# Product keys in eight stages instead of five, with every engine's order written out

## The chip, the cores and the metric

The kernel runs on one core of a Trainium2 chip. The core has five engines that work side by side, each through its own list of instructions in order: PE (TensorE, matmuls and transposes), DVE (VectorE), ACT (ScalarE), POOL (GpSimd), and SP (SyncE), which here only issues transfers. Instructions on different engines wait for each other by semaphores. The metric is the device time of one execution in microseconds (us), lower is better. Matmuls write to a memory of their own, PSUM, of eight banks; all other tiles stand in SBUF.

## The reference

A model of four layers, each a gated cross attention and a gated feed-forward block, on 16 sequences of 128 tokens and width 256. All arithmetic is in float32. The change lies in the last block, a feed-forward layer of product keys:

```
q  = batch_norm(x @ Wq + bq)            # 8 heads x (2 halves of 32)
q0, q1 = l2norm(first half), l2norm(second half)
s0, s1 = q0 . k0, q1 . k1               # 32 scores each
ts0, ti0 = top_k(s0, 4);  ts1, ti1 = top_k(s1, 4)
w  = softmax over all 16 sums ts0[i] + ts1[j]
idx = ti0[i] * 32 + ti1[j]              # one of 256 experts
out = sum over heads and pairs of  up[idx] * w * gelu(down[idx] . x)
```

All 16 pairs are kept, so the softmax over the sums is the product of two softmaxes, one over the four best of each half. Indices that would reach past the 256 experts (first index 8 or more) use the last expert.

## The kernel before

The kernel works on 16 tiles of 128 tokens (one sequence each). The last block is `attention_ffn3` (L1178). It first computes all queries, their batch-norm statistics, and `eh`, the gelu of every expert's down product, for all tiles. That ends with `gain` and `shift` (L1277 to L1280). Then comes the part that is changed: a loop over the 16 tiles.

For one tile `b` it does the following. ACT makes the squares and the normalised queries of four blocks (L1293, L1294). PE sums the squares by head half (`pn`, L1297), DVE copies the 16 sums out of PSUM (`rn`, L1299), and POOL takes the root with a power instruction and keeps it from zero (L1300, L1301). PE multiplies the queries with the keys (`ps`, L1304), and ACT copies the 16 x 32 scores to one of three score tiles (L1306). DVE inverts the norms (L1313); ACT takes 16 exps, one for each head half, with the inverted norm as the scale (`wgt`, L1316).

The four best of 32 scores are found on DVE in two steps for each of the 16 head halves. The eight largest come from a maximum instruction (L1320). The places 4 to 7 are overwritten by one memset with a value that stands behind the scores (L1321). Then a match instruction (L1324) marks, in a copy `rep`, where the remaining values stand. A scalar_tensor_tensor (L1328) keeps the exps at the marked places and zeroes the others.

Then the weights: sums over each half (`tot`, L1330), their reciprocal (L1331), the product of both halves' reciprocals (`both`, L1335), the scaled first eight weights of the first half (`w0`, L1337; the profile calls it `w`), the sum of the other 24 (`far`, L1339), scaled (L1340), and summed over the heads (`rest`, L1342). POOL multiplies `w0` with the 32 weights of the second half, for 8 heads x 8 x 32 products (`pr`, L1344). PE adds the eight heads by multiplying with the identity (`we`, L1355, with `rest` put to the last expert, L1359). DVE multiplies with `eh` (`ew`, L1361). PE turns the result (L196), ACT copies it (`eT`, L197), PE applies the up weights (`po`, L1369), DVE adds it with the gate to the tile (L236), and SP writes the tile out (L1371).

The loop is written as five stages a tile apart: `score(t)`, `pick(t - 2)`, `mix(t - 3)`, `apply(t - 4)`. In this loop a planner orders the instructions of each engine by when it expects their inputs, so the order on the chip is not that of the source. Other loops of the kernel already stand in a block where each engine takes its instructions in the order of the source, for PE, ACT, DVE and POOL (L613).

Of the kernel before, what the change touches and what calls it, by code (L numbers as in the profile page):

```python
# [12 lines left out]
F32 = mybir.dt.float32  # L13
I32 = mybir.dt.int32
BF16 = mybir.dt.bfloat16
AF = mybir.ActivationFunctionType
# [3 lines left out]
P = 128  # L20
B, S, D = 16, 128, 256
NH = 16
NG, GT = 4, 512
ENGINES = {mybir.EngineType.PE, mybir.EngineType.Activation, mybir.EngineType.DVE, mybir.EngineType.Pool}
# [9 lines left out]
def flamingo_gated(ctx: ExitStack, tc: tile.TileContext, a, out):  # L34
    nc = tc.nc
# [9 lines left out]
    def bank(name):  # L45
        return psum.tile([P, 512], F32, tag="ps", name=name)
# [20 lines left out]
    def gate_f(layer):  # L67
        return gates[:, 4 + layer : 5 + layer]
# [123 lines left out]
    def transposed(src, dst):  # L192

        pt = bank("pt")
        for c in range(2):
            nc.tensor.transpose(pt[:, c * P : (c + 1) * P], src[:, c * P : (c + 1) * P], ident)  # L196
        nc.scalar.copy(dst, pt[:, 0:256].rearrange("p (c t) -> p c t", c=2))  # L197

    class Norm:
# [17 lines left out]
        def turn(self, b):  # L217
            transposed(self.rows.pop(b), self.into(b))
# [16 lines left out]
    def add_gated(b, ps, gate):  # L235
        nc.vector.scalar_tensor_tensor(xb[b], ps, gate, xb[b], ALU.mult, ALU.add)  # L236
# [941 lines left out]
    def attention_ffn3():  # L1178
        norm, xnT = norm_stage()
        attention3(after=[norm.whole])  # L1180
        with ExitStack() as es:
            kp = es.enter_context(tc.tile_pool(name="pk", bufs=1))
            pp = es.enter_context(tc.tile_pool(name="pw", bufs=2))
# [3 lines left out]
            wu = wt[:, 1536:2048].rearrange("p (c m) -> p c m", c=2)  # L1187
# [13 lines left out]
            blk = kp.tile([P, 4], F32, name="blk")  # L1201
# [30 lines left out]
            for g in range(NG):  # L1232
                q = kp.tile([P, 4, GT], F32, tag=f"q{g}", name=f"q{g}")
                for c in range(4):
                    pq = bank("pq")
                    for k in range(2):
                        nc.tensor.matmul(  # L1237
                            pq, lhsT=wq[:, k, c * P : (c + 1) * P], rhs=xnT[g][:, k, :], start=(k == 0), stop=(k == 1)
# [10 lines left out]
            for b in range(B):  # L1249
                pe = bank("pe")  # L1250
                for k in range(2):
                    nc.tensor.matmul(
                        pe[:, 0:D], lhsT=xnT[b // 4][:, k, b % 4 * S : (b % 4 + 1) * S], rhs=wd[:, k, :],
                        start=(k == 0), stop=(k == 1),
                    )
                t = kp.tile([P, D], F32, tag=f"eh{b}", name="eh")
# [18 lines left out]
            gain = kp.tile([P, 1], F32, name="gain")  # L1275
            rsqrt(gain, var, 1e-5)
            nc.vector.tensor_tensor(gain, gain, par[:, 4:5], ALU.mult)  # L1277
            shift = kp.tile([P, 1], F32, name="shift")
# [4 lines left out]
            scored = [kp.tile([P, 16, 36], F32, tag=f"sc{i}", name=f"sc{i}") for i in range(3)]  # L1283
            for t in scored:
                nc.gpsimd.memset(t[:, :, 32:36], SENT)
            raw, norms, picked, mixed = {}, {}, {}, {}

            def score(b):

                q = qT[b // 4][:, :, (b % 4) * S : (b % 4 + 1) * S]  # L1290
                both = ctxp.tile([P, 2, 4, S], F32, tag="ctxT", name="both")
                q2, qn = both[:, 0], both[:, 1]
                nc.scalar.activation(q2, q, AF.Square, bias=shift, scale=gain)  # L1293
                nc.scalar.activation(qn, q, AF.Identity, bias=shift, scale=gain)  # L1294
                pn = bank("pn")
                for c in range(4):
                    nc.tensor.matmul(pn[:, c * 4 : (c + 1) * 4], lhsT=q2[:, c, :], rhs=blk, start=True, stop=True)  # L1297
                rn = pp.tile([P, 16], F32, tag="rn", name="rn", bufs=3)
                nc.vector.tensor_copy(rn, pn[:, 0:16])  # L1299
                nc.gpsimd.tensor_tensor(rn, rn, half.to_broadcast([P, 16]), ALU.pow)  # L1300
                nc.gpsimd.tensor_scalar(rn, rn, 1e-12, 1.0, ALU.max, ALU.mult)  # L1301
                ps = bank("ps")
                for c in range(4):
                    nc.tensor.matmul(ps[:, c * P : (c + 1) * P], lhsT=qn[:, c, :], rhs=kdT, start=True, stop=True)  # L1304
                sc = scored[b % 3]
                nc.scalar.copy(sc[:, :, 0:32], ps.rearrange("p (g k) -> p g k", k=32))  # L1306
                raw[b], norms[b] = sc, rn

            def pick(b):


                rn, sc = norms.pop(b), raw.pop(b)
                nc.vector.reciprocal(rn, rn)  # L1313
                w = pp.tile([P, 16, 32], F32, tag="wgt", name="wgt", bufs=3)
                for h in range(16):
                    nc.scalar.activation(w[:, h, :], sc[:, h, 0:32], AF.Exp, scale=rn[:, h : h + 1])  # L1316

                best = pp.tile([P, 16, 8], F32, tag="best", name="best")
                for h in range(16):
                    nc.vector.max(out=best[:, h, :], in_=sc[:, h, :])  # L1320
                nc.vector.memset(best[:, :, 4:8], SENT)  # L1321
                rep = pp.tile([P, 16, 36], F32, tag="rep", name="rep", bufs=1)
                for h in range(16):
                    nc.vector.match_replace(  # L1324
                        out=rep[:, h, :], in_to_replace=best[:, h, :], in_values=sc[:, h, :], imm_value=FOUND
                    )

                nc.vector.scalar_tensor_tensor(w, rep[:, :, 0:32], FOUND, w, ALU.is_equal, ALU.mult)  # L1328
                tot = pp.tile([P, 16], F32, tag="tot", name="tot")
                nc.vector.tensor_reduce(tot, w, AX.X, ALU.add)  # L1330
                nc.vector.reciprocal(tot, tot)  # L1331
                wv = w.rearrange("p (h s) k -> p h s k", s=2)
                tv = tot.rearrange("p (h s) -> p h s", s=2)
                both = pp.tile([P, 8], F32, tag="both", name="both")
                nc.vector.tensor_tensor(both, tv[:, :, 0], tv[:, :, 1], ALU.mult)  # L1335
                w0 = pp.tile([P, 8, 8], F32, tag="w0", name="w0")
                nc.vector.tensor_tensor(w0, wv[:, :, 0, 0:8], both.unsqueeze(2).to_broadcast([P, 8, 8]), ALU.mult)  # L1337
                far = pp.tile([P, 8], F32, tag="far", name="far")
                nc.vector.tensor_reduce(far, wv[:, :, 0, 8:32], AX.X, ALU.add)  # L1339
                nc.vector.tensor_tensor(far, far, tv[:, :, 0], ALU.mult)  # L1340
                rest = pp.tile([P, 1], F32, tag="rest", name="rest", bufs=3)
                nc.vector.tensor_reduce(rest, far, AX.X, ALU.add)  # L1342
                pr = pp.tile([P, 8, 8, 32], F32, tag="pr", name="pr")
                nc.gpsimd.tensor_tensor(  # L1344
                    pr, w0.unsqueeze(3).to_broadcast([P, 8, 8, 32]),
                    wv[:, :, 1, :].unsqueeze(2).to_broadcast([P, 8, 8, 32]), ALU.mult,
                )
                picked[b] = pr, rest

            def mix(b):  # L1350

                pr, rest = picked.pop(b)
                we = bank("we")
                for h in range(8):
                    nc.tensor.matmul(  # L1355
                        we[:, 0:D], lhsT=ident, rhs=pr[:, h].rearrange("p i k -> p (i k)"), start=(h == 0), stop=(h == 7)
                    )
                    if h == 0:
                        nc.tensor.matmul(we[:, D - 1 : D], lhsT=ident, rhs=rest, start=False, stop=False)  # L1359
                ew = pp.tile([P, D], F32, tag="ew", name="ew")  # L1360
                nc.vector.tensor_tensor(ew, eh[b], we[:, 0:D], ALU.mult)  # L1361
                mixed[b] = ew

            def apply(b):
                eT = pp.tile([P, 2, P], F32, tag="eT", name="eT")
                transposed(mixed.pop(b), eT)
                po = bank("po")
                for k in range(2):
                    nc.tensor.matmul(po[:, 0:D], lhsT=eT[:, k, :], rhs=wu[:, k, :], start=(k == 0), stop=(k == 1))  # L1369
                add_gated(b, po[:, 0:D], gate_f(3))  # L1370
                nc.sync.dma_start(out=out[b], in_=xb[b])  # L1371

            for t in range(B + 4):
                if 2 <= t < B + 2:
                    pick(t - 2)
                if t < B:
                    score(t)
                if 3 <= t < B + 3:
                    mix(t - 3)
                if t >= 4:  # L1380
                    apply(t - 4)


    def attention1(after, joining):
# [43 lines left out]

    attention_ffn2(attention_ffn1(attention_ffn0()))
    attention_ffn3()  # L1430


# [94 lines left out]
```

## Time and profile before

| | |
|---|---|
| median of 3 runs | 2210.04 us (2206.56 to 2211.8) |
| the profiled execution | 2212.79 us |
| its span in the trace | 2211.1 us |
| first square of the changed loop (L1293) | 2034.53 us |
| mean TensorE clock over the span | 0.936 |
| busy over the span: PE, DVE, ACT, POOL | 1948.9, 1291.9, 957.7, 769.3 us |

The page shows the whole program, of which the changed loop is the last 176.6 us. The busy times of the page are therefore of little use here; the loop has to be read from a window over its own stretch. In lines of a group or of the timeline, `rn<-pn` means that tile `rn` is written and `pn` read; x16 is the number of instructions, and an arrow in brackets names what ended the engine's idle time before the instruction. Where a query gives three durations, they are the shortest, the median and the longest in ns.

### The profile page before, as it was taken

The page shows a single profiled execution, that of the slowest core. Times are in us where ns is not written, and L with a number is a line of the kernel's source. Part 1 is how long each engine was busy: PE and PEld are TensorE (multiplying, and loading weights), DVE is VectorE, ACT ScalarE, POOL GpSimd, SP SyncE. Part 2 cuts the span into 40 slices and gives each one's busy share as a digit, 9 for nine tenths or more (in the row PEclk, how much of TensorE's full clock was granted, in tenths as well). Part 3 has the DMA queues.
Part 4 walks back from the last instruction along what each step waited for, and adds up shares of the span by engine and source line. Part 5 has one row for each costly group of instructions (what it writes and reads, how often), then busy time and mean ns, then how long its engine had stood idle before and what let it go on. Part 6 is the DMA issues. An engine that isn't in the chain of part 4 may idle for free.

```text
span 2211.1 us, 31775 instructions
## 1 busy us (share of the span) xinstructions
PE 1948.9 (88%) x10603; PEld 1319.0 (60%) x10603; DVE 1291.9 (58%) x3965; ACT 957.7 (43%) x3103; POOL 769.3 (35%) x921
## 2 busy tenths in 40 slices
PE   5996999888859999978887998949899999988787
PEld 4774566566645666655664444438776777765676
DVE  3776122267773222227766999859926667652775
ACT  5884222288851122228872111134424344434662
POOL 3653333255430145535543222200011222221675
PEclk9998999989879999999998999979999999999788
DMA  2002777511012288873002113543210000000000
GB/s 91 33 23 80 301 293 294 179 37 34 26 30 88 98 311 320 314 261 122 25 18 108 67 76 143 189 168 114 77 39 1 11 11 1 20 2 0 8 13 20
DMA packets 56563, 223.48 MB, mean 101 GB/s; under 512 B 11984, under 2 KB 31952, under 8 KB 44240
## 3 DMA queue, kind: packets, MB, share of 16 engines
q0 software_dynamic: 15312, 134.10, 16.6%
q1 hardware_dynamic: 41088, 87.36, 11.4%
q8 instruction: 84, 1.38, 0.3%
q14 instruction: 79, 0.65, 0.1%
HBM read 190.24 MB, written 31.20 MB: 100 GB/s over the span
## 4 chain that ended last, share of the span: by engine, by line
PE 25%; DVE 19%; POOL 4%; issue 4%; ACT 3%; DMA 1%; POOLq 0%; ACTq 0%; SPq 0%; DVEq 0%
PE pk L266 3%; PE pq L278 2%; PE po L361 2%; PE pv L289 2%; DVE tot L1135 2%; POOL rn L1300 2%; PE po L1155 2%; DVE d L1082 1%; DVE red L1079 1%; DVE tot L1086 1%; PE av L351 1%; DVE cw L1129 1%; PE sc L308 1%; PE pq L1237 1%; DVE cw L1137 1%
## 5 line engine op out<-in xcount | busy, mean ns | idle before, releaser
L803 PE MATMUL pg<-we,xT 128*128 128x512 f32 (+1 forms) x588 | 268.2, 586 | 1.0 <-ACT xT L197 1.0
L538 POOL TENSOR_TENSOR e<-e,sums 128x512 f32<-128x512 f32 x192 | 194.1, 1043 | 144.4 <-DVE sums L533 106.9
L809 DVE TENSOR_TENSOR h<-sg,pg 128x256 f32<-128x256 f32 x147 | 60.3, 411 | 248.0 <-ACT sg L808 201.8
L808 ACT ACTIVATE sg<-pg 128x256 f32<-128x256 f32 x147 | 55.3, 376 | 303.0 <-PE pg L803 295.5
L525 ACT ACTIVATE e<-sc,mx 128x128 f32<-128x128 f32 x512 | 179.7, 413 | 0.0
L803 PEld LDWEIGHTS pg<-we,xT 128*128 128x128 f32 x588 | 106.2, 192 | 89.1 <-issue 79.1
L778 POOL DMA_INDIRECT we<-in_we,rows x62 | 60.0, 967 | 264.3 <-PE pd L834 172.7
L834 PE MATMUL pd<-we,hT 128*128 128x256 f32 (+1 forms) x588 | 141.7, 383 | 1.2 <-ACT hT L823 1.2
L329 POOL TENSOR_TENSOR e<-e,rec 128x512 f32<-128x512 f32 x64 | 65.3, 1041 | 216.7 <-DVE rec L328 140.3
L834 PEld LDWEIGHTS pd<-we,hT 128*128 128x128 f32 (+1 forms) x588 | 109.6, 190 | 44.1 <-issue 25.8
L1155 PE MATMUL po<-yt,cT 128*128 128x256 f32 x512 | 128.2, 396 | 8.5 <-ACT cT L1147 8.4
L1098 PE MATMUL acc<-d,k 128*128 128x512 f32 x256 | 122.4, 620 | 9.7 <-POOL d L1088 9.5
L525 ACT ACTIVATION_READ_ACCUMULATOR e<-sc,mx 128x1 f32 x512 | 129.4, 253 | 0.0
L1088 POOL TENSOR_TENSOR d<-d,tot 128x1024 f32<-128x1024 f32 x32 | 62.8, 1961 | 168.4 <-DVE tot L1087 168.4
L494 PE MATMUL sc<-kT,qT 32*128 32x256 f32 x768 | 98.3, 432 | 25.0 <-DVE v L438 14.0
L1083 ACT ACTIVATE d<-d 128x1024 f32<-128x1024 f32 x32 | 33.8, 1057 | 195.5 <-DVE d L1082 189.2
L1072 PE MATMUL pl<-phi,xnT 128*128 128x512 f32 x256 | 116.5, 599 | 0.0
L544 PE MATMUL pe<-ident,e 128*128 128x128 f32 x768 | 104.1, 289 | 10.4 <-POOL e L538 10.2
L1155 PEld LDWEIGHTS po<-yt,cT 128*128 128x128 f32 x512 | 97.4, 200 | 21.4 <-ACT cT L1147 9.7
L180 POOL TENSOR_SCALAR ve<-mv 128x1 f32<-128x1 f32 (+1 forms) x136 | 26.1, 192 | 234.2 <-DVE mv L187 183.4
L544 PEld LDWEIGHTS pe<-ident,e 128*128 128x128 f32 x768 | 92.0, 152 | 17.2 <-POOL e L538 15.5
L236 DVE SCALAR_TENSOR_TENSOR x<-po,gates,x 128x256 f32<-128x256 f32 x96 | 45.4, 473 | 91.5 <-PE po L361 53.2
(291 smaller groups left out, 4538.4 us busy)
## 6 DMA issues: line engine op xcount, KB each, us to landing
ew<-in_ew SPq DMA_DIRECT2D x8, 2048.0 KB
spill<-lg SPq DMA_DIRECT2D x32, 512.0 KB
cw<-spill SPq DMA_DIRECT2D x8, 2048.0 KB
ctxT<-in_ctxT SPq DMA_DIRECT2D x16, 512.0 KB
got<-results SPq DMA_DIRECT2D x48, 128.0 KB
normed<-xn SPq DMA_DIRECT2D x32, 128.0 KB
aw<-in_aw SPq DMA_DIRECT2D x3, 1280.0 KB
x<-in_x SPq DMA_DIRECT2D x16, 128.0 KB
```

What stands on the lines that cost most here:

```text
L266: nc.tensor.matmul(pk, lhsT=wk[:, k, c * P : (c + 1) * P], rhs=ctxT[g][:, k, :], start=(k == 0), stop=(k == 1))
L329: nc.gpsimd.tensor_tensor(e, e, rec.unsqueeze(2).to_broadcast([P, 4, S]), ALU.mult)
L494: nc.tensor.matmul(banks[j][:, c * 256 : (c + 1) * 256].rearrange("p (i k) -> p i k", i=2), lhsT=qT[r, c, tok], rhs=kT[r, c, :, tok], star ...
L525: nc.scalar.activation(e[:, c, :], sc[:, c, :], AF.Exp, bias=mx[:, h : h + 1], scale=sign, accum_out=sums[b][:, h : h + 1],)
L538: nc.gpsimd.tensor_tensor(e, e, r, ALU.mult)
L544: nc.tensor.transpose(pe[:, c * P : (c + 1) * P], e[:, c, :], ident)
L803: nc.tensor.matmul(pg[:, 0 : 2 * m].rearrange("p (g i) -> p g i", g=2), lhsT=tokens[j][:, k, :], rhs=wgu[:, k, :, i0 : i0 + m], start=(k = ...
L834: nc.tensor.matmul(pd[:, 0:D], lhsT=hT[0:m, ic, :], rhs=wd[0:m, ic, :], start=(ic == 0), stop=(ic == nic - 1))
L1072: nc.tensor.matmul(pl, lhsT=xnT[b // 4][:, k, tok], rhs=phi[:, k, n], start=(k == 0), stop=(k == 1))
L1088: nc.gpsimd.tensor_tensor(dv, dv, tot.unsqueeze(2).to_broadcast([P, 32, 32]), ALU.mult)
L1098: nc.tensor.matmul(acc[hf][k][q], lhsT=keep[b][:, k * P : (k + 1) * P], rhs=d[:, q * 512 : (q + 1) * 512], start=(b == 0), stop=(b == B - 1),)
L1155: nc.tensor.matmul(pos[b][:, 0:D], lhsT=cT[:, c, :], rhs=yt[2 * q + c // 2][:, c % 2, :], start=(q == 0 and c == 0), stop=(q == 3 and c == 3),
```

## The change

The loop's four functions become eleven, which run up to seven turns apart, and the loop is put in a block in which PE, ACT, DVE and POOL each take their instructions in the order of the source. In turn `t` a stage with lag `k` works on tile `t - k`. The order of the table is the order in the turn.

Nothing is computed differently. `score` is split into `square`, `norm_sums`, `root` and `products`; `pick` into `exps`, `best_four` and `weigh`; `apply` into `turn`, `project` and `leave`. `rep`, in which the four best are marked, gets two buffers in place of one, `best` one in place of two, and `wgt` two in place of three. In `weigh` the instructions from L1328 to the end of `pick` are kept in their order of the source.

```diff
-            def score(b):
+            def square(b):
...
+            def norm_sums(b):
...
                 nc.vector.tensor_copy(rn, pn[:, 0:16])
+                norms[b] = rn
+
+            def root(b):
+                rn = norms[b]
                 nc.gpsimd.tensor_tensor(rn, rn, half.to_broadcast([P, 16]), ALU.pow)
                 nc.gpsimd.tensor_scalar(rn, rn, 1e-12, 1.0, ALU.max, ALU.mult)
+
+            def products(b):
...
-            def pick(b):
-                rn, sc = norms.pop(b), raw.pop(b)
+            def exps(b):
+                rn = norms.pop(b)
                 nc.vector.reciprocal(rn, rn)
-                w = pp.tile([P, 16, 32], F32, tag="wgt", name="wgt", bufs=3)
+                w = pp.tile([P, 16, 32], F32, tag="wgt", name="wgt")
...
+            def best_four(b):
+                sc = raw.pop(b)
-                best = pp.tile([P, 16, 8], F32, tag="best", name="best")
+                best = pp.tile([P, 16, 8], F32, tag="best", name="best", bufs=1)
...
-                rep = pp.tile([P, 16, 36], F32, tag="rep", name="rep", bufs=1)
+                rep = pp.tile([P, 16, 36], F32, tag="rep", name="rep")
...
+            def weigh(b):
+                w, rep = found.pop(b)
                 nc.vector.scalar_tensor_tensor(w, rep[:, :, 0:32], FOUND, w, ALU.is_equal, ALU.mult)
...
-            for t in range(B + 4):
-                if 2 <= t < B + 2:
-                    pick(t - 2)
-                if t < B:
-                    score(t)
-                if 3 <= t < B + 3:
-                    mix(t - 3)
-                if t >= 4:
-                    apply(t - 4)
+            stages = (
+                (2, root), (6, turn), (3, exps), (7, leave), (4, weigh), (1, norm_sums), (1, products),
+                (3, best_four), (5, mix), (6, project), (0, square),
+            )
+            with tc.manual_schedule(engines=ENGINES):
+                for t in range(B + 7):
+                    for lag, stage in stages:
+                        if 0 <= t - lag < B:
+                            stage(t - lag)
```

More of the change, by code (lines that the diff above doesn't have):

```diff
@@ L1285, in attention_ffn3 @@
                 nc.gpsimd.memset(t[:, :, 32:36], SENT)
-            raw, norms, picked, mixed = {}, {}, {}, {}
-            def score(b):
+            squares, norms, raw, found, picked, mixed, turned, outs = {}, {}, {}, {}, {}, {}, {}, {}
+            def square(b):
                 q = qT[b // 4][:, :, (b % 4) * S : (b % 4 + 1) * S]
                 both = ctxp.tile([P, 2, 4, S], F32, tag="ctxT", name="both")
-                q2, qn = both[:, 0], both[:, 1]
-                nc.scalar.activation(q2, q, AF.Square, bias=shift, scale=gain)
-                nc.scalar.activation(qn, q, AF.Identity, bias=shift, scale=gain)
+                nc.scalar.activation(both[:, 0], q, AF.Square, bias=shift, scale=gain)
+                nc.scalar.activation(both[:, 1], q, AF.Identity, bias=shift, scale=gain)
+                squares[b] = both
+            def norm_sums(b):
                 pn = bank("pn")
                 for c in range(4):
-                    nc.tensor.matmul(pn[:, c * 4 : (c + 1) * 4], lhsT=q2[:, c, :], rhs=blk, start=True, stop=True)
+                    nc.tensor.matmul(pn[:, c * 4 : (c + 1) * 4], lhsT=squares[b][:, 0, c, :], rhs=blk, start=True, stop=True)
                 rn = pp.tile([P, 16], F32, tag="rn", name="rn", bufs=3)
                 nc.vector.tensor_copy(rn, pn[:, 0:16])
+                norms[b] = rn
+            def root(b):
+                rn = norms[b]
                 nc.gpsimd.tensor_tensor(rn, rn, half.to_broadcast([P, 16]), ALU.pow)
                 nc.gpsimd.tensor_scalar(rn, rn, 1e-12, 1.0, ALU.max, ALU.mult)
+            def products(b):
+                qn = squares.pop(b)[:, 1]
                 ps = bank("ps")
@@ L1306, in score @@
                 nc.scalar.copy(sc[:, :, 0:32], ps.rearrange("p (g k) -> p g k", k=32))
-                raw[b], norms[b] = sc, rn
-            def pick(b):
-                rn, sc = norms.pop(b), raw.pop(b)
+                raw[b] = sc
+            def exps(b):
+                rn = norms.pop(b)
                 nc.vector.reciprocal(rn, rn)
-                w = pp.tile([P, 16, 32], F32, tag="wgt", name="wgt", bufs=3)
+                w = pp.tile([P, 16, 32], F32, tag="wgt", name="wgt")
                 for h in range(16):
-                    nc.scalar.activation(w[:, h, :], sc[:, h, 0:32], AF.Exp, scale=rn[:, h : h + 1])
-                best = pp.tile([P, 16, 8], F32, tag="best", name="best")
+                    nc.scalar.activation(w[:, h, :], raw[b][:, h, 0:32], AF.Exp, scale=rn[:, h : h + 1])
+                found[b] = w
+            def best_four(b):
+                sc = raw.pop(b)
+                best = pp.tile([P, 16, 8], F32, tag="best", name="best", bufs=1)
                 for h in range(16):
@@ L1326, in pick @@
                     )
+                found[b] = found[b], rep
+            def weigh(b):
+                w, rep = found.pop(b)
                 nc.vector.scalar_tensor_tensor(w, rep[:, :, 0:32], FOUND, w, ALU.is_equal, ALU.mult)
@@ L1362, in mix, with turn, project, leave @@
                 mixed[b] = ew
[L1364 to L1367, printed above, removed]
+            def turn(b):
+                turned[b] = pp.tile([P, 2, P], F32, tag="eT", name="eT")
+                transposed(mixed.pop(b), turned[b])
+            def project(b):
+                eT = turned.pop(b)
+                outs[b] = bank("po")
                 for k in range(2):
-                    nc.tensor.matmul(po[:, 0:D], lhsT=eT[:, k, :], rhs=wu[:, k, :], start=(k == 0), stop=(k == 1))
-                add_gated(b, po[:, 0:D], gate_f(3))
+                    nc.tensor.matmul(outs[b][:, 0:D], lhsT=eT[:, k, :], rhs=wu[:, k, :], start=(k == 0), stop=(k == 1))
+            def leave(b):
+                add_gated(b, outs.pop(b)[:, 0:D], gate_f(3))
                 nc.sync.dma_start(out=out[b], in_=xb[b])
-            for t in range(B + 4):
-                if 2 <= t < B + 2:
-                    pick(t - 2)
-                if t < B:
-                    score(t)
-                if 3 <= t < B + 3:
-                    mix(t - 3)
-                if t >= 4:
-                    apply(t - 4)
+            stages = (
[7 more added lines that the diff above has]
+                            stage(t - lag)
     def attention1(after, joining):
```

## The prediction

> **What bounds the kernel now.** I read the page first (span 2211.1 us), then the chain of waits, which shows that the change touches only the last stage: its first instruction that moves, the squares of L1293, starts at 2034.53 us, and everything before stays as it is. Then the busy times of that stretch, its waits, and its timeline on VectorE (DVE) and GpSimd (POOL).
>
> The stage's busy times (columns: window, length, then busy us of PE, PE loads, DVE, ACT, POOL, then granted clock), and its two longest waits (us in all, times, longest):
>
> ```profile
> 2034.50:2211.10 176.60, 136.08 (x640) 117.77 (x640) 118.69 (x976) 94.05 (x321) 108.91 (x48) 0.82 0.04 13
> ...
> POOL rn L1300 <- DVE rn L1299: 36.1, 14, 5.3
> DVE rn L1313 <- POOL rn L1301: 34.5, 15, 3.4
> ```
>
> No engine is full: DVE is busy 118.7 of 176.6 us, PE 136.1 at a clock of 0.82. What ends the time is a ring between two engines. One tile of it, from the timeline (start, length):
>
> ```profile
> 2127.59 0.16 DVE L1299 COPY rn<-pn 128x16 f32<-128x16 f32 x1
> 2127.71 0.22 DVE L1337 TENSOR_TENSOR w<-wgt,both 128x64 f32<-128x64 f32 x1
> 2127.84 2.94 POOL L1300 TENSOR_TENSOR rn<-rn,half 128x16 f32<-128x16 f32 x1 [2.45 <-DVE rn L1299]
> 2127.85 0.16 DVE L1340 TENSOR_TENSOR far<-far,tot 128x8 f32<-128x8 f32 x1
> ...
> 2131.10 3.64 POOL L1344 TENSOR_TENSOR pr<-w,wgt 128x2048 f32<-128x2048 f32 x1
> 2131.17 0.25 DVE L1313 RECIPROCAL rn<-rn 128x16 f32<-128x16 f32 x1 [2.12 <-POOL rn L1301]
> ```
>
> DVE copies a norm, POOL takes its root (2.94 + 0.28 us), DVE waits 2.12 us for it, works through one tile, and copies the next norm. POOL's roots start at 2118.52, 2127.84 and 2137.09: 9.3 us a tile. Note where POOL's long product `pr` (3.64 us) falls: beside DVE's maxima and matches, after DVE has finished `far` (L1340) and `w0` (shown as w, L1337).
>
> **The change, part by part.** (1) Root two stages ahead. `root(b)` now runs one turn after its copy and one before its reciprocal, so the ring is gone. That is worth DVE's 34.5 us of waiting, unless something takes the place. (2) DVE's order as written. In one turn DVE now does: reciprocal, add of an older tile, `weigh`, norm copy, 16 maxima, 16 matches, `ew`. Nothing is interleaved any more, so the small dependent steps follow each other bare. Start-to-start times from the timeline, 0.03 us added after an instruction whose result the next needs: reciprocal 0.22, add 0.39, the scalar_tensor_tensor 0.72, `tot` 0.72, its reciprocal 0.28, `both` 0.20: `w0` starts 2.53 us into the turn. After it: `far`'s sum 0.14 later, 0.34 long, then L1340 and `rest`, copy, maxima 1.59, memset 0.11 with two gaps, matches 2.64, `ew` 0.33.
>
> (3) The step that decides. `w0` now stands ahead of `far` on DVE, as in the source; in all 16 tiles of before the L1340 product stands ahead of `w0` or beside the root. POOL's `pr` needs `w0` and `wgt` only. How soon it starts, with POOL idle, is seen at the end of the stage:
>
> ```profile
> 2194.05 0.16 DVE L1340 TENSOR_TENSOR far<-far,tot 128x8 f32<-128x8 f32 x1
> 2194.24 0.23 DVE L1337 TENSOR_TENSOR w<-wgt,both 128x64 f32<-128x64 f32 x1
> 2194.38 0.15 DVE L1342 TENSOR_REDUCE rest<-far 128x1 f32<-128x8 f32 x1
> ...
> 2194.63 3.63 POOL L1344 TENSOR_TENSOR pr<-w,wgt 128x2048 f32<-128x2048 f32 x1 [5.62 <-DVE rest L1342]
> ```
>
> `pr` starts 0.39 us after `w0`'s start (0.38 at 2185.38). In the new order L1340 can start only 0.14 + 0.34 + 0.03 = 0.51 us after it (0.46 with the shortest `far` of 0.29). So `pr` is running when L1340 comes, by 0.07 to 0.13 us. And L1340 reads two operands from SBUF. What such a DVE instruction does beside a POOL product:
>
> ```profile
> 1330.10 1.92 POOL L1088 TENSOR_TENSOR d<-d,tot 128x1024 f32<-128x1024 f32 x1
> 1330.17 1.86 DVE L1020 SCALAR_TENSOR_TENSOR nm<-mv,rs 128x2 f32<-128x2 f32 x1 [0.32 <-POOL rs L181]
> ...
> L1020 DVE SCALAR_TENSOR_TENSOR nm<-mv,rs x8: 151/160/1861, 1330.2 to 1457.5; 128x2 f32<-128x2 f32 x8
> L667 DVE TENSOR_TENSOR cum<-cum,mask x16: 167/171/961, 83.0 to 205.7; 128x8 f32<-128x8 f32 x16
> ...
> 2052.84 3.64 POOL L1344 TENSOR_TENSOR pr<-w,wgt 128x2048 f32<-128x2048 f32 x1 [3.70 <-DVE rest L1342]
> 2055.90 1.13 DVE L1328 SCALAR_TENSOR_TENSOR wgt<-rep,wgt 128x512 f32<-128x512 f32 x1
> ```
>
> L1020 came 0.07 us behind the POOL product and lasted 1861 ns instead of 160: it ended with it. L667, of L1340's very size, once took 961 instead of 171. L1328, met by `pr` itself, took 1.13 instead of 0.68. Instructions with one SBUF operand beside `pr` keep their times (reciprocal 0.25, matches 0.18). So in each turn L1340 should last until `pr` ends: `w0` + 0.38 + 3.64 + 0.02 = 4.04 us after `w0`'s start in place of 0.67, and everything on DVE stands behind it.
>
> The turn is then 2.53 + 4.04 + 0.03 + `rest` 0.08 + copy 0.08 + maxima and memset 1.76 + matches 2.64 + `ew` 0.33 = 11.49 us; without the block 8.12.
>
> POOL's root beside such instructions costs nothing: `far` took 0.16 at 2127.85 just behind the root. [...]
>
> (4) Other edits. `wgt` 3 to 2 buffers: the exps write the one that `pr` of the turn before read, done 5 us earlier; `best` 2 to 1 and `rep` 1 to 2 are written and read on DVE alone, in order. Banks: five a turn of eight; `po` waits one turn for its add, three banks remain. Cost nothing as long as a turn is over 8 us. ACT's turn: 2 x 0.71 + 0.48 + 16 x 0.21 + 0.27 = 5.6 us, and one table load as before. POOL's: 3.02 + 0.24 + 3.64 = 6.9. The output DMAs (SP) leave three turns later, one a turn; the last ends 2.9 us after the last add, as now. PE: at full clock 0.81 (L1297), 0.97 (L1304), 3.7 (L1355), 0.4, 0.97 (L1369) = 6.8 us a turn; at half clock 1.56, 1.85, 7.2, 0.4, 1.87 = 12.9. Its results are needed at the turn's end (`ew`), 11.1 us after the previous one: even at half clock throughout, turn, norms, products and mix take 11.0. Priced at nothing, with up to 1.4 us a turn kept for the range.
>
> (5) Fill. Square 0 at 2034.53; the score loop ACT-PE-ACT takes about 5 us a tile at the half clock that the trace shows here; so norm copy 2 falls at 2046.8, maxima and matches of tile 0 end at 2051.3 and `pr` 0 starts at 2054.2 (2052.84 now). (6) The turns. Turn 4 from 2051.3, without add and `ew`, 10.8; turns 5 and 6, without add, 11.1 each; so turn 7 starts at 2084.3; 12 full turns of 11.49 bring 2222.2; the last `pr` ends 6.3 later, 2228.5. (7) Drain: from the last `pr`'s end to the end of the span 12.8 us now (2198.3 to 2211.1), with the same work in it. Sum: 2241.3, against 2211.1: +30 us.
>
> The profiled execution took 2212.79 us (1.7 around its span); the median of the runs is 2210.04, so 2.7 lower. Against the median: 2241.
>
> **The rivals.** *No block, and faster.* If `pr` came after L1340, each turn is 8.12: turns 4 to 6 take 22.9, twelve 97.4, last `pr` end 2177.9, span 2190.7; about 2190, and up to 2202 if PE's clock holds the 8 us turn up by a microsecond. For it: the profile names `rest`, not `w0`, as `pr`'s releaser, and `pr` starts 0.08 to 0.10 after `rest`'s end, the gap at which POOL's root follows the norm copy. Against it: `pr` reads nothing that `rest` writes, 0.15 to 0.17 us after `w0`'s end is as regular, and a margin of 0.07 us was enough at L1020. It decides if `pr` starts over 0.5 us after `w0`. *Blocked in part.* With the block in half the turns, 2216. *PE becomes the bound too.* PE would idle 4 us in each blocked turn; in the trace L1369's four matmuls took 2.08 us in place of 1.13 at 2114.65, behind an idle of 2.56 us, and an idle of 7.07 us was followed by half speed until about 2094. [...] With half clock throughout a turn is 12.9: 14 x 1.4 = +20, 2261. Against it: after the 7.07 us, PE was back at full speed within 8.5 us of work.
>
> **How the numbers follow.** Blocked, DVE the bound: 80 in 100, 2232 to 2250 (0.3 us a turn either way over 14 turns, and 4 for fill and drain). Blocked with PE holding it further: 5, to 2262. Blocked in part: 4, around 2216, of which 2 within 0.2% (4.4 us, about what this kernel's runs can tell from no change). No block: 11, faster. So faster 0.11, same 0.02, slower 0.87; the range 2226 to 2260 leaves out the no-block case and a few of the others.
>
> **What would show it.** Right: L1340 at about 3.5 us in place of 0.158 in 16 of 16, starting about 0.1 us after `pr`; DVE's waits for L1301 gone; `pr` starts 11.5 us apart; POOL idle before `pr` waiting for DVE. Wrong: L1340 at 0.16, and `pr` starts 8 to 9 us apart; or DVE waiting for L1355 in most turns.

## The result and the profile after

The changed kernel takes 2241.19 us (median of 4 runs, 2237.97 to 2245.05), the kernel before 2210.92 (4 runs, 2206.56 to 2212.72). The ratio is 1.0139, with a 95% interval of 1.012 to 1.0158: it is slower by 30 us.

The lines of the source have moved: the product on `far` that was L1340 is now L1355, `w0` L1352, `far`'s sum L1354, `pr` L1359, the root L1305, the norm's reciprocal L1320. The changed loop runs in the profiled execution from 2031.15 us, its first square, to the end of the span, 2236.3. That is 205.1 us in place of 176.6, so the loop alone accounts for 28.6 of the 30 us.

First the loop's window in the kernel after (busy us of PE, PE loads, DVE, ACT, POOL, then the granted clock), and under it the waits of DVE and one of POOL's (us in all, times, longest):

```profile
2031.10:2236.30 205.20, 147.26 (x640) 127.29 (x640) 179.65 (x976) 92.31 (x321) 109.08 (x48) 0.76 0.03 11
...
DVE rn L1300 <- PE pn L1298: 12.0, 3, 5.0
DVE ew L1376 <- PE we L1370: 3.8, 1, 3.8
...
POOL pr L1359 <- DVE w L1352: 69.0, 15, 7.8
```

DVE's waits for the root, 34.5 us before, are gone; the ring is broken, as the change meant. What is left of DVE's waits lies in the fill and in the last two tiles. But DVE is now busy 179.65 us instead of 118.69 with the same 976 instructions. They did not become more, so some became longer. POOL now idles 69 us in front of `pr`, waiting for `w0`.

One turn of the timeline of the kernel after (start, length), and its 16 products on `far`, under those of the kernel before (shortest, median, longest in ns):

```profile
2141.21 0.23 DVE L1352 TENSOR_TENSOR w<-wgt,both 128x64 f32<-128x64 f32 x1
2141.35 0.34 DVE L1354 TENSOR_REDUCE far<-wgt 128x8 f32<-128x192 f32 x1
2141.61 3.64 POOL L1359 TENSOR_TENSOR pr<-w,wgt 128x2048 f32<-128x2048 f32 x1 [4.22 <-DVE w L1352]
2141.73 3.54 DVE L1355 TENSOR_TENSOR far<-far,tot 128x8 f32<-128x8 f32 x1
2145.30 0.16 DVE L1357 TENSOR_REDUCE rest<-far 128x1 f32<-128x8 f32 x1
...
L1340 DVE TENSOR_TENSOR far<-far,tot x16: 153/159/161, 2052.2 to 2194.1; 128x8 f32<-128x8 f32 x16
L1355 DVE TENSOR_TENSOR far<-far,tot x16: 3508/3536/3541, 2050.8 to 2221.9; 128x8 f32<-128x8 f32 x16
```

`pr` starts 0.40 us behind `w0`. The product on 128 x 8 numbers comes 0.12 us behind `pr` and ends with it, 3.54 us later, where it took 0.159 before. This happens in 16 of 16 tiles. The extra time is 16 x 3.38 = 54 us. The durations of all other DVE instructions add up to what they did before (174.8 and 175.0 us); but in the written order they overlap less, so that DVE's busy time rises by 61.0 us in all. Its idle time in the loop falls by 32.4 us, from 57.9 to 25.5, since the waits for the root are gone. The difference is the 28.6 us by which the loop is longer.

### The profile page after: what moved, and what is told of

Its sections match the earlier page's. It is cut to its first block, busy times and chain, and to the rows that moved or that the text cites. A ratio compares the mean times of both kernels' runs of the same rounds, so it can differ in the third digit from the quotient of the medians.

```text
span 2236.3 us, 31823 instructions
## 1 busy us (share of the span) xinstructions
PE 1953.8 (87%) x10603; PEld 1323.4 (59%) x10603; DVE 1352.5 (60%) x3965; ACT 955.5 (43%) x3103; POOL 769.3 (34%) x921
## 4 chain that ended last, share of the span: by engine, by line
PE 25%; DVE 22%; issue 3%; ACT 3%; POOL 2%; DMA 1%; SPq 0%; ACTq 0%; POOLq 0%; DVEq 0%
DVE far L1355 3%; PE pk L266 2%; PE pq L278 2%; PE po L361 2%; PE pv L289 2%; DVE tot L1135 2%; PE acc L1098 2%; DVE rep L1335 2%; PE pl L1072 2%; PE po L1155 2%; PE av L351 1%; DVE cw L1129 1%; PE sc L308 1%; PE pq L1237 1%; DVE cw L1137 1%
## 5 line engine op out<-in xcount | busy, mean ns | idle before, releaser
L1155 PEld LDWEIGHTS po<-yt,cT 128*128 128x128 f32 x512 | 95.5, 196 | 23.9 <-ACT cT L1147 12.8
L525 ACT ACTIVATE e<-e,mx 128x128 f32<-128x128 f32 x256 | 98.8, 389 | 0.0
```

The source lines that it names most:

```text
L525: nc.scalar.activation(e[:, c, :], sc[:, c, :], AF.Exp, bias=mx[:, h : h + 1], scale=sign, accum_out=sums[b][:, h : h + 1],)
L1155: nc.tensor.matmul(pos[b][:, 0:D], lhsT=cT[:, c, :], rhs=yt[2 * q + c // 2][:, c % 2, :], start=(q == 0 and c == 0), stop=(q == 3 and c == 3),
```

## The experiments

The theory (A) is that the product is held because it reads two operands from SBUF while POOL's `pr` runs. The rivals are that its place or the long written order costs the time whatever the operands (B), and that PE's speed would bind the loop anyway (C). The first four kernels ran on one chip beside 16 runs of the kernel before (2212.39 us), the last three on one beside 15 (2214.00).

**`w0` behind `rest`.**

```diff
-                nc.vector.tensor_tensor(w0, wv[:, :, 0, 0:8], both..., ALU.mult)
                 nc.vector.tensor_reduce(far, wv[:, :, 0, 8:32], AX.X, ALU.add)
                 nc.vector.tensor_tensor(far, far, tv[:, :, 0], ALU.mult)
                 nc.vector.tensor_reduce(rest, far, AX.X, ALU.add)
+                nc.vector.tensor_tensor(w0, wv[:, :, 0, 0:8], both..., ALU.mult)
```

> The changed kernel with `w0` written behind `rest`, so that both instructions of `far` and `rest` are done before POOL is released. Theory A (the far product lasts 3.5 us because it reads two SBUF operands while `pr` runs): it falls to 0.16 us in all 16 tiles, a turn falls from 11.49 to about 8.1 us (0.17 + 0.30 + 0.72 + 0.72 + 0.29 + 0.14 + 0.38 + 0.19 + 0.08 + 0.14 + 0.08 + 4.52 + 0.33 = 8.06), and the time by some 15 x 3.4 = 51 us to about 2190; up to 2202 if PE's clock holds single turns up. Theory B (the long order as written is itself what costs, the block only fills a wait that would be there anyway): the far product becomes short, but another wait of about 3 us takes its place, the time stays above 2225. Theory C (PE takes over): turns of 9 us and more, DVE waits for L1370's matmuls or L1387's, 2205 or more.

Measured: 2191.64 us (2191.0 to 2194.25), ratio to before 0.9913 (0.9891 to 0.9935). The loop takes 154.6 us. From the lines of this kernel, the product on `far`, the scalar_tensor_tensor that comes beside the root, and DVE's waits:

```profile
L1353 DVE TENSOR_TENSOR far<-far,tot x16: 166/168/170, 2054.1 to 2175.1; 128x8 f32<-128x8 f32 x16
L1343 DVE SCALAR_TENSOR_TENSOR wgt<-rep,wgt x16: 630/680/693, 2051.9 to 2172.9; 128x512 f32<-128x512 f32 x16
...
DVE ew L1376 <- PE we L1370: 6.5, 2, 3.6
DVE x L236 <- PE po L1387: 3.4, 7, 1.4
```

One instruction moved behind three others, and the change turns from 30 us slower to 21 us faster. `pr` starts are 8.0 us apart, in some turns 8.55, where DVE waits for PE's `po`; those waits are 3.4 us in all, so C is a small correction. No other wait of about 3 us a turn takes the place of the held product, so the long written order by itself is not what costs (the second half of B). Whether the product is held for its place behind `w0` is left to the next run.

**One operand in PSUM, the order unchanged.**

```diff
                 far = pp.tile([P, 8], F32, tag="far", name="far")
-                nc.vector.tensor_reduce(far, wv[:, :, 0, 8:32], AX.X, ALU.add)
-                nc.vector.tensor_tensor(far, far, tv[:, :, 0], ALU.mult)
+                sums = bank("pf")[:, 0:8]
+                nc.vector.tensor_reduce(sums, wv[:, :, 0, 8:32], AX.X, ALU.add)
+                nc.vector.tensor_tensor(far, sums, tv[:, :, 0], ALU.mult)
```

> The changed kernel in its own order, but the sum of `far` goes to a PSUM bank, so that the far product has one SBUF operand in place of two and still comes 0.1 us behind the start of `pr`. Theory A: it is not held up, lasts about 0.2 us, and the turn falls to 8.1 to 8.3 us, the time to 2190 to 2203. Theory B (what holds it is its place behind `w0`, any DVE instruction there would wait for POOL, or a semaphore): it stays at 3.5 us and the time at 2241.

Measured: 2196.73 us (2190.41 to 2200.09), ratio 0.9927 (0.9898 to 0.9956). A turn of its timeline on both engines, and its products:

```profile
2099.40 3.63 POOL L1360 TENSOR_TENSOR pr<-w,wgt 128x2048 f32<-128x2048 f32 x1 [1.27 <-DVE w L1352]
2099.53 0.17 DVE L1356 TENSOR_TENSOR far<-pf,tot 128x8 f32<-128x8 f32 x1
...
L1356 DVE TENSOR_TENSOR far<-pf,tot x16: 165/166/167, 2059.4 to 2181.8; 128x8 f32<-128x8 f32 x16
```

The product stands at the same place, 0.13 us behind the start of `pr`, and is not held in any tile (0.165 to 0.167 us). So it is neither the place nor a semaphore, but where the operands lie. A turn is 8.13 us, as A expects. This tells A from B most directly.

**The same order under POOL's root.** The norm copy moves into the stage of the root, and that stage to just ahead of `weigh`, so that POOL is in its root when `w0` is ready.

```diff
+            def root(b):
+                rn = pp.tile([P, 16], F32, tag="rn", name="rn", bufs=3)
+                nc.vector.tensor_copy(rn, norms[b][:, 0:16])
...
-                (2, root), (6, turn), (3, exps), (7, leave), (4, weigh), ...
+                (6, turn), (3, exps), (7, leave), (2, root), (4, weigh), ...
```

> The changed kernel with the norm copy moved to the stage of the root, and that stage to just ahead of `weigh`: the order `both`, `w0`, far sum, far product, `rest` is kept, but POOL is in its root (2.9 us) when they come, and `pr` starts only after it, about 3.8 us into the turn in place of 2.9. Theory A with a root that does not hold DVE (as the trace of before shows): the far product lasts 0.16 us, beside the root; a turn of 8.1 to 8.3 us, 2190 to 2203. [...] Theory B: no change, 2241.

Measured: 2205.32 us (2197.7 to 2210.51, 7 runs), ratio 0.9963 (0.9944 to 0.9983). Its timeline in one turn with a root and in one without, and the durations of root and product:

```profile
2092.00 3.27 POOL L1305 TENSOR_TENSOR rn<-rn,half 128x16 f32<-128x16 f32 x1 [0.88 <-DVE rn L1303]
2094.28 0.17 DVE L1355 TENSOR_TENSOR far<-far,tot 128x8 f32<-128x8 f32 x1
2095.60 3.64 POOL L1359 TENSOR_TENSOR pr<-w,wgt 128x2048 f32<-128x2048 f32 x1
...
2176.99 3.63 POOL L1359 TENSOR_TENSOR pr<-w,wgt 128x2048 f32<-128x2048 f32 x1 [2.97 <-DVE w L1352]
2177.11 3.54 DVE L1355 TENSOR_TENSOR far<-far,tot 128x8 f32<-128x8 f32 x1
...
L1305 POOL TENSOR_TENSOR rn<-rn,half x16: 2897/3277/3308, 2042.6 to 2166.8; 128x16 f32<-128x16 f32 x16
L1355 DVE TENSOR_TENSOR far<-far,tot x16: 166/168/3535, 2058.7 to 2188.4; 128x8 f32<-128x8 f32 x16
```

In the turns with a root the product slips in beside it and takes 0.17 us. In three tiles POOL is idle when `w0` comes, and there the product is held again (3.51 to 3.54 us): in the first, where DVE waits 3.41 us for the exps and the root is over by then, and in the last two, for which no root is left to run. The expectation, 2203 at most, was missed by 2 us; it had not thought of those three tiles, which cost 3 x 3.37 = 10 us. The comparison within one kernel shows that `pr` has to be running: a root does not hold the product.

**Eight stages without the written order.** Only the block that fixes the order is taken out.

```diff
-            with tc.manual_schedule(engines=ENGINES):
-                for t in range(B + 7):
+            for t in range(B + 7):
...
```

> The changed kernel's eleven stages without the block that fixes the order: the planner orders the engines again. Theory A: the planner puts far's product ahead of `w0` or under the root in most tiles, few or none are held, and without the ring the turns are 8 to 9.3 us: 2190 to 2212. If the order as written is not what brings the block (theory B): the far product is held here too, 2230 or more.

Measured: 2210.93 us (2205.57 to 2218.3, 10 runs), ratio 0.9994 (0.9977 to 1.001). Its products on `far`, its scalar_tensor_tensors, and what DVE and ACT wait for:

```profile
L1355 DVE TENSOR_TENSOR far<-far,tot x16: 152/158/162, 2053.1 to 2187.9; 128x8 f32<-128x8 f32 x16
L1343 DVE SCALAR_TENSOR_TENSOR wgt<-rep,wgt x16: 627/682/3309, 2051.0 to 2184.3; 128x512 f32<-128x512 f32 x16
...
DVE rn L1320 <- POOL rn L1306: 26.2, 16, 3.4
...
ACT wgt L1323 <- POOL pr L1359: 42.8, 12, 9.3
```

No product on `far` is held, as A expects. The scalar_tensor_tensor, which also reads two SBUF operands, meets `pr` in four tiles and takes 0.91 to 3.31 us there in place of 0.68; the planner's order does not avoid every such meeting. And the finer stages, with their two `wgt` buffers, bring nothing alone: the planner puts the norm's reciprocal again right where its root is not done (26.2 us of waits, 34.5 before), and ACT's exps now wait for the `pr` that still reads one of the two `wgt` buffers. How much of that a third buffer would give back was not tried.

**The written order without the eight stages.** The kernel before, its loop put in the block, and `w0` behind `rest`.

```diff
-            for t in range(B + 4):
-                if 2 <= t < B + 2:
-                    pick(t - 2)
+            with tc.manual_schedule(engines=ENGINES):
+                for t in range(B + 4):
+                    if 2 <= t < B + 2:
+                        pick(t - 2)
...
```

> The kernel before with its five stages and buffers, each engine's order as written (pick, score, mix, apply in one turn), and `w0` behind `rest` as in far_first: the written order without the finer staging. If the order as written is what gains, it comes near far_first's 2192. If the eight stages are needed for it, the turn is one long chain over engines: reciprocal, exps on ACT (3.7 us), squares (0.8), norms and scores on PE (2.0), mix (3.7), turn, eT and po (2.0), add (0.4): 12.6 us a turn, 3.3 more than before's 9.3, so 16 x 3.3 = 53 us more: about 2250 to 2265.

Measured: 2283.73 us (2280.18 to 2286.66), ratio 1.03 (1.0275 to 1.0326). Its longest waits on DVE, and PE's:

```profile
DVE ew L1361 <- PE we L1355: 79.3, 15, 6.4
DVE x L236 <- PE po L1369: 21.0, 15, 1.4
...
PE pn L1297 <- ACT both L1293: 75.3, 16, 6.2
```

The long chain over the engines is there as expected, but a turn takes 15.5 us (`pr` starts at 2092.01 and, 11 turns later, at 2262.03), not 12.6. The expectation had PE at full clock; in this loop the granted clock is 0.72. In the steady turns PE takes 1.87 us for the norms and 2.05 for the scores, where the faster tiles of before took 0.95 and 1.14, and the mix 4.4 to 5.8 us in place of 3.84: together 2.4 to 3.8 us, about what the expectation was short of. As these two kernels stand, neither part of the change gains alone: the stages without the order give nothing, the order without the stages costs 70 us.

**`pr` in two halves.** The changed kernel with `far` in its own place, so that the product is still met by POOL.

```diff
+                for i in range(0, 8, 4):
                     nc.gpsimd.tensor_tensor(
-                        pr, ...
+                        pr[:, i : i + 4], w0[:, i : i + 4]..., wv[:, i : i + 4, 1, :]..., ALU.mult,
```

> The changed kernel with `pr` made in two POOL instructions of four heads each (about 1.85 us each) in place of one of 3.64. If a held DVE instruction gets in between two POOL products, the far product lasts about 1.75 us, a turn is 9.7 us, and the time falls by 15 x 1.8 = 27 us to about 2214. If the second product follows so closely that DVE is passed over (in the trace of before L953 lay beside the end of one product and all of the next), it lasts 3.5 us or more and the time stays at 2241 to 2244.

Measured: 2219.87 us (2213.85 to 2229.37, 10 runs), ratio to before 1.0025 (1.0007 to 1.0043). From its timeline, and its products:

```profile
2139.99 3.78 POOL L1360 TENSOR_TENSOR pr<-w,wgt 128x1024 f32<-128x1024 f32 x2 [2.77 <-DVE w L1352]
2140.11 1.81 DVE L1355 TENSOR_TENSOR far<-far,tot 128x8 f32<-128x8 f32 x1
...
L1355 DVE TENSOR_TENSOR far<-far,tot x16: 1784/1809/1811, 2062.2 to 2208.8; 128x8 f32<-128x8 f32 x16
```

Half the POOL instruction, half the stall (1.78 to 1.81 us in place of 3.51 to 3.54): the price here follows the length of what POOL does, and DVE gets its turn between the halves. The loop falls from 205.1 to 178.7 us, by 26.4 where 27 were expected; the whole time is 6 us above the number given. The kernel before, too, is 3 us longer beside this run (2214.00 us) than beside the changed kernel (2210.92). The part ahead of the loop is the same program in all of them, and its length differs between executions (first square at 2030.2 to 2042.8 in these profiles), so of the other 3 us no more can be said.

**Independent instructions between dependent ones.** `w0` stays behind the product; `weigh` and `best_four` are split so that independent instructions stand between dependent ones, and the squares come first in the turn.

```diff
+            stages = (
+                (0, square), (2, root), (6, turn), (4, keep), (3, exps), (4, sums), (1, norm_sums), (1, products),
+                (4, heads), (3, maxima), (7, leave), (3, matches), (5, mix), (6, project),
+            )
```

Here `keep` is the scalar_tensor_tensor, `sums` the two sums and the reciprocal, `heads` the rest of `weigh` in the order `both`, far product, `w0`, `rest`, `pr`; `maxima` and `matches` are the two halves of `best_four`.

> A version meant to beat far_first: `w0` behind the far product; `weigh` and `best_four` split, so that between two DVE instructions of which one needs the other stands an independent one (norm reciprocal, norm copy, far sum, the add), and the squares first in the turn. Start to start by far_first's own rows: some 0.6 to 0.7 us less on DVE, a turn of 7.3 to 7.5 us in place of 8.0; PE needs 6.8 us at full clock and 7.5 at a mean of 0.9, so it should be the next bound. 2178 to 2186. If PE's clock falls further or DVE waits for L1370's results in most turns, no better than far_first: 2189 to 2195.

Measured: 2179.59 us (2173.18 to 2181.31, 5 runs), ratio to before 0.9828 (0.9805 to 0.9851). Its loop's window, and two neighbouring `pr` from POOL's timeline:

```profile
2038.40:2179.60 141.20, 122.44 (x640) 106.83 (x640) 119.13 (x976) 93.19 (x321) 108.51 (x48) 0.89 0.05 16
...
2106.74 3.64 POOL L1354 TENSOR_TENSOR pr<-w,wgt 128x2048 f32<-128x2048 f32 x1 [0.51 <-PE ps L1313]
2114.12 3.64 POOL L1354 TENSOR_TENSOR pr<-w,wgt 128x2048 f32<-128x2048 f32 x1 [0.53 <-PE ps L1313]
```

A turn is 7.38 us, and the time is below far_first's, whose ratio to the kernel before on its own chip was 0.9913. PE, DVE and POOL are busy 122, 119 and 109 of 141 us; POOL waits only half a microsecond ahead of `pr` (the profile names PE's `ps`, which `pr` does not read). The expectation had PE as the next bound. But in the steady turns, from 2080 to 2150 us, DVE is busy 69.63 of 70 us and waits for nothing, with PE busy 63.94 us at a granted clock of 1.00: DVE still sets the turn.

## Why the prediction was right, point by point

*The ring goes.* Right: DVE's 34.5 us of waits for the root are gone from the changed kernel.

*`pr` overtakes the far product by 0.07 to 0.13 us.* Right: 0.12 in the turn shown, 0.12 to 0.15 over the 16 tiles. This was the step with the least room. It held since both times are regular: `pr` starts 0.38 to 0.40 us behind `w0`'s start (0.38 to 0.39 read from before), and the product 0.52 to 0.53 behind it (0.51 reckoned).

*The product is held to the end of `pr`.* Right, 3.54 us in place of the 3.53 that follow from the prediction's times (4.04 less 0.51). The prediction took this from three other instructions of the trace; far_psum and under_root show that both conditions it named, two SBUF operands and a running product on POOL, are needed here: with one of them missing the product takes 0.17 us.

*The turn.* 11.49 us predicted; most `pr` starts are 11.49 to 11.50 apart (2130.11 to 2141.61). That it fits to the hundredth is luck, since single terms were off and cancelled: the first reciprocal and the add take 0.17 and 0.30 from start to start in place of 0.22 and 0.39, and the maxima with the memset 1.87 in place of 1.76.

*Buffers, banks, PE.* Nothing waits for them in the steady turns. PE's clock fell to 0.76 in the loop (0.82 before), short of the half clock throughout that the rival needed, and DVE waits for `ew` only once, in the last tile. So that rival did not come to bear.

*Fill and drain.* The first `pr` starts 19.5 us behind the first square (19.7 predicted), and the drain takes 10.9 us in place of 12.8: it had been copied from before, where the last 14 matmuls of the last mix took 4.95 us, in place of 3.27 in the kernel after. In all the loop was predicted at 206.8 us and took 205.1.

*The total.* That 2241 and 2241.19 agree to 0.2 us is in part luck. The sum's own last step gives 2240.2 (2241.3 for the span, less the 1.1 us by which the median of before lies under its span), which the prediction wrote as 2241. The loop was 1.7 us shorter than predicted, and the part ahead of it alone differs by several microseconds between executions.

*The no-block rival* would have given 2190 to 2202: far_first, which is that case made on purpose, took 2191.64, with turns of 8.0 us where 8.12 were reckoned. The rival's ground, that the profile names `rest` as `pr`'s releaser, was a name put to the last event ahead of the start; the changed kernel's profile names `w`.

## What to carry to other kernels

When an order is written out by hand, look at what an instruction sets free on the other engines, and at what stands right behind it on its own. Here the DVE product with two SBUF operands belonged ahead of the instruction that releases the long POOL product, or needed one operand in PSUM: it took 0.17 us in both cases, 3.54 otherwise. A planner's order may avoid such a meeting without anyone having asked for it, as it did for the product on `far` in 16 of 16 tiles of before, and it may also bring one about, as it did for the scalar_tensor_tensor L1328: in 5 of those tiles `pr` still had 0.34 to 0.58 us to run when it came, and it took 0.89 to 1.13 us in place of 0.68. So a loop that is put in written order should be read again for such meetings. In this loop only the staging and the order together gained, with `w0` behind `rest`; as tried here, each alone gave nothing or cost 70 us.

## What the runs showed of the hardware

A tiny DVE instruction can be held for as long as POOL's: 0.12 us of lead made 0.17 into 3.54 us, and 1.81 with POOL's product halved. Between the two halves DVE got its turn in 16 of 16 tiles, though in the trace of before one instruction (L953, 1.08 us) lay beside the end of one product and the whole of the next.

POOL's root does not hold such instructions: in far_first the scalar_tensor_tensor comes 1.0 to 2.1 us behind the start of a root in 13 tiles, with 0.8 to 1.9 us of the root (2.91 us) still to run, and keeps its time in all of them (0.63 to 0.69 us, as where no root runs). But the root itself takes longer when it comes second: in under_root, where it starts 0.16 us behind that instruction in 13 tiles, it takes 3.27 to 3.31 us in place of 2.90 to 2.92. What makes the root differ from `pr` in this was not tried.
